# Attention values from a per-image table of column strips in DRAM

## The chip, the cores and the metric

The kernel runs on one core of one Trainium2 chip. A core has TensorE (PE; PEld is its loading of weights), VectorE (DVE), ScalarE (ACT), GpSimd (POOL) and SyncE (SP), which here only issues DMAs; each works through its own instruction queue in order, and they wait for each other by semaphores. The metric is device time in microseconds, as the median of several runs.

## What is computed

Two layers on an image batch x of 2 x 256 x 48 x 48, all in fp32. Layer 0 is a local attention beside a small convolution, on the group-normalised image; layer 1 is a Mamba block and a top-2 mixture of 8 experts on the tokens. The change touches the attention of layer 0 alone:

```python
q = (_c1x1(x, Wq, bq) * HD ** (-0.5)).reshape(b * HEAD, HD, n)
k = _c1x1(x, Wk, bk).reshape(b * HEAD, HD, h, w)
v = _c1x1(x, Wv, bv).reshape(b * HEAD, HD, h, w)
uk = _unfold(jnp.pad(k, rpad, mode='reflect'), KA).reshape(b * HEAD, HD, kk, n)
uv = _unfold(jnp.pad(v, rpad, mode='reflect'), KA).reshape(b * HEAD, HD, kk, n)
att = jnp.einsum('bdn,bdkn->bnk', q, uk + upe[None])
att = jax.nn.softmax(att, axis=-1)
out_att = jnp.einsum('bnk,bdkn->bdn', att, uv).reshape(b, c, h, w)
...
return rate1 * out_att + rate2 * out_conv
```

Every pixel attends to the 7 x 7 window around it (KA = 7), with 4 heads of 64 channels. Since the softmax weights of a pixel add up to 1, the bias bv of the values adds rate1 * bv to each result.

## The kernel before

**Layer 0, one image after the other** (`layer0_image`). `group_norm` writes the normalised image, reflected by 3 pixels on each side, into two tiles `xp` of 128 channels x 54 x 54 (DVE at L221, POOL for the borders at L227 to L232; the reciprocal root `grstd` is POOL's, L162). Matmuls at L272 and L287 make queries and keys, ACT (L277) and DVE (L291) take them out of PSUM.

**Blocks and rounds.** The 48 x 48 queries are cut into 18 blocks of 8 x 16; a block's keys are a window of 14 x 22 = 308 positions of the padded image. `attend` handles a block: POOL copies the block's window of `xp` into a dense tile `win` (L311, once per channel half); PE projects it by Wv in three pieces of 110, 110 and 88 positions (L319), DVE adds the bias on the way out of PSUM into `val` (L323); PE makes the scores of a head pair (L331), DVE adds the mask and takes the maximum (L337); ACT exponentiates (L345), DVE scales by 1/sum and rate1 (L352); for each head pair PE transposes the probabilities (L360), ACT copies them out as `pt` (L364, L367), PE multiplies by `val` (L374), and DVE adds the result into x (L379).

**What sets the order.** Three blocks go through these steps side by side, together with the convolution (`conv_steps`: 36 taps per image of about 2.5 us each on DVE, L248 and L250; half of them write `hid`, half add into x). `interleave` steps all four streams in turn, and six such rounds make an image. The generators give the program order; a scheduler then writes each engine's queue, reordering what does not depend on each other. Taps that add into x and the results at L379 write the same tile, so they keep their program order.

**Buffers.** `bank` is a pool of four PSUM banks (projections, results of L374), `banks` one of two double banks (scores and transposed probabilities in turn). `win`, `val`, `prob` and `pt` have three buffers (NATT). One program matmul in fp32 shows as two records in the trace.

After layer 0 come `mamba` (both images interleaved) and `experts`, which the change does not touch.

Of the kernel before, what the change touches and what calls it, by code (L numbers as in the profile page):

```python
# [40 lines left out]
HP = H + 2 * PAD  # L41
QR, QC = 8, 16
KR, KC = QR + 2 * PAD, QC + 2 * PAD
NKEY = KR * KC
KCH = ((0, 5), (5, 5), (10, 4))
NRB, NCB = H // QR, W // QC
NATT = 3
NEG = -3.0e38

DI, DS, SH = 512, 64, 8  # L50
# [6 lines left out]
E, HID = 8, 1024  # L57
# [12 lines left out]
_VEC = {}  # L70
_n = 0
for _name, _k in (
    ("bq", NH), ("bk", NH), ("bp", 1), ("w1", NH * 9), ("w2", NH * 9), ("norm_w", NH),
    ("gnorm_w", DI // P), ("conv_w", NM * 4), ("conv_b", NM),
):
    _VEC[_name] = (_n, _n + _k)
    _n += _k
# [2 lines left out]
_ROW = {}  # L80
_n = 0
for _name, _k in (
    ("bv", C), ("dt_bias", SH), ("A_log", SH), ("Dp", SH), ("bg", E), ("rate1", 1), ("rate2", 1),
):
    _ROW[_name] = (_n, _n + _k)
    _n += _k
# [32 lines left out]
class Kernel:  # L119
# [45 lines left out]
    def layer0(self, ctx):  # L165
        nc, ins, v, r = self.nc, self.ins, self.v, self.r
        wts = self.pool("l0w", 1, ctx)
        self.xpp = self.pool("xpp", 1, ctx)
        self.att = self.pool("att", NATT, ctx)
        w = {}  # L170
        for k in ("Wq", "Wk", "Wv"):
            w[k] = wts.tile([P, NH, C], F32, name=k)
            nc.scalar.dma_start(w[k], ins[k].rearrange("(h p) o -> p h o", p=P))
        wp = wts.tile([2, P], F32, name="wp")
        nc.scalar.dma_start(wp, ins["Wp"])
        pos = self.xpp.tile([2, HP, HP], F32, tag="kp0", name="pos")
        nc.scalar.dma_start(pos, ins["pos"].rearrange("a (r c) -> a r c", r=HP))

        bq8 = wts.tile([P, NH], F32, name="bq8")
        nc.vector.tensor_scalar(bq8, v["bq"], HD ** -0.5, None, ALU.mult)  # L180
        bkp = wts.tile([P, NH], F32, name="bkp")
        nc.vector.tensor_scalar(bkp, v["bk"], v["bp"], None, ALU.add)
        w2r = wts.tile([P, NH * 9], F32, name="w2r")
        nc.vector.tensor_scalar(w2r, v["w2"], r["rate2"], None, ALU.mult)


        pe = wts.tile([P, HP, HP], F32, name="pe")
        for g in range(6):
            ps = self.bank()
            nc.tensor.matmul(ps[:, : 9 * HP], lhsT=wp, rhs=pos[:, 9 * g : 9 * g + 9, :], start=True, stop=True)  # L190
            nc.scalar.copy(pe[:, 9 * g : 9 * g + 9, :], ps[:, : 9 * HP].rearrange("p (r c) -> p r c", r=9))
        self.l0 = dict(w, bq8=bq8, bkp=bkp, w2r=w2r, pe=pe)
        for b in range(B):
            self.layer0_image(b)
            if b == 0:
                self.scale_weights()
# [65 lines left out]
    def layer0_image(self, b):  # L262
# [3 lines left out]
        for h in range(NH):  # L266
# [28 lines left out]
                )  # L295
            kp.append(kh)

        def blocks(first):
            for i in range(first, NRB * NCB, NATT):
                yield from self.attend(b, i // NCB, i % NCB, xp, q, kp)  # L300

        interleave(*[blocks(i) for i in range(NATT)], self.conv_steps(b, xp))

    def attend(self, b, rb, cb, xp, q, kp):

        nc, l0, att = self.nc, self.l0, self.att
        r0, c0 = rb * QR, cb * QC

        win = att.tile([P, NH, NKEY], F32, tag="win", name="win")
        for k in range(NH):  # L310
            nc.gpsimd.tensor_copy(  # L311
                win[:, k, :].rearrange("p (r c) -> p r c", r=KR), xp[k][:, r0 : r0 + KR, c0 : c0 + KC]
            )
        val = att.tile([P, len(KCH), C], F32, tag="val", name="val")
        for i, (kr, nr) in enumerate(KCH):
            ps = self.bank()
            nk = nr * KC
            for k in range(NH):
                nc.tensor.matmul(  # L319
                    ps[:nk, :C], lhsT=win[:, k, kr * KC : (kr + nr) * KC], rhs=l0["Wv"][:, k, :],  # L320
                    start=k == 0, stop=k == NH - 1,
                )
            nc.vector.tensor_tensor(val[:nk, i, :], ps[:nk, :C], self.r["bv"][:nk, :], ALU.add)  # L323

        prob = att.tile([P, 4, NKEY], F32, tag="prob", name="prob")
        top = self.small.tile([P, 4], F32, tag="top", name="top")
# [27 lines left out]
        for h in range(NH):  # L354
# [24 lines left out]
            nc.vector.tensor_tensor(x, po[:, :P].rearrange("p (r c) -> p r c", r=QR), x, ALU.add)  # L379


    def mamba(self, ctx):
# [468 lines left out]
    def run(self):  # L851
# [8 lines left out]
                nc.sync.dma_start(self.x[b][:, h, :], self.ins["x"][b, h * P : (h + 1) * P, :])  # L860
        self.mamba_weights()
        self.xs = nc.dram_tensor("xs", (NROWS, XW), F32).ap()
        self.acc = nc.dram_tensor("acc", (B * N + P, C), F32).ap()

        self.none = self.const.tile([P, XW], F32, name="none")
# [47 lines left out]
def _arrays(i):  # L913
# [5 lines left out]
    cols = lambda a: a.reshape(-1, P).T  # L919
    taps = lambda a, k: a.reshape(-1, P, k).transpose(1, 0, 2).reshape(P, -1)  # L920
    vec = {
        "bq": cols(l0("bq")), "bk": cols(l0("bk")), "bp": cols(np.tile(l0("bp"), 2)),
        "w1": taps(l0("w1"), 9), "w2": taps(l0("w2"), 9), "norm_w": cols(at("norm_w")),
        "gnorm_w": cols(at("gnorm_w")), "conv_w": taps(at("conv_w"), 4), "conv_b": cols(at("conv_b")),
    }
# [3 lines left out]
         np.broadcast_to(ff("b2")[:, None, :], (E, P, C)),  # L929
         np.broadcast_to(np.eye(E, dtype=np.float32)[:, None, :], (E, P, E))], axis=2)  # L930
    row = {
        "bv": l0("bv"), "dt_bias": at("dt_bias"), "A_log": at("A_log"), "Dp": at("Dp"), "bg": ff("bg"),
        "rate1": l0("rate1").reshape(1), "rate2": l0("rate2").reshape(1),
    }
    out = {
# [27 lines left out]
```

## Time and profile before

| | us |
|---|---|
| median of 3 runs | 2132.05 (2126.8 to 2132.95) |
| the profiled execution's own time | 2135.79 |
| its span in the trace | 2133.7 |
| PE busy in the span | 1745.8 (82%) |
| DVE busy | 1071.7 (50%) |
| POOL busy | 660.3 (31%) |
| ACT busy | 628.7 (29%) |
| granted TensorE clock, mean | 0.859 of full |
| image 0: first Wv matmul to last result | 80.8 to 264.2 |
| image 1: first Wv matmul to last result | 323.8 to 506.6 |
| last tap of layer 0 ends | 517.0 |

How to read the views: a group's row gives the line, engine, operation and tile names, the shapes and the count, then busy time in us and mean ns of one, then how long the engine sat idle just before these instructions and what ended most of that wait. A timeline row gives start and length in us, and in brackets the idle time ahead of it with its releaser. A row of windows gives busy time of each engine in a stretch. DMA rows give the count, the KB of each and the median time from issue to landing.

In layer 0, up to 28 us the inputs are loaded; after that hardly any DMA runs until the Mamba stage.

### The profile page before, as it was taken

To read this page: it belongs to the slowest core of one execution; us is meant where nothing else is said; L and a number is where in the kernel's file an instruction comes from. 1 tells how busy PE (TensorE), PEld (TensorE's weight loads), DVE (VectorE), ACT (ScalarE), POOL (GpSimd) and SP (SyncE) were. 2 spreads that over 40 slices of the span, in tenths; PEclk is the share of its full clock that TensorE was granted. 3 is DMA by queue.
4 is the path that set the end of the run, shared out by engine and by line. 5 is a ranking of instruction groups with operands and counts; after the bars stand their busy time and mean duration, and the time that the engine had idled before them with its cause. 6 is when DMAs were issued, how large, how long until landed. Compare 5 with 4: busy or idle time off the path is not lost. (4 is left out here: it accounts for less than half of the span.)

```text
span 2133.7 us, 22277 instructions
## 1 busy us (share of the span) xinstructions
PE 1745.8 (82%) x7928; PEld 1267.9 (59%) x7928; DVE 1071.7 (50%) x2673; ACT 628.7 (29%) x1449; POOL 660.3 (31%) x579
## 2 busy tenths in 40 slices
PE   5988779785988878887788789339999999999993
PEld 2556536563555554554555545228888888888883
DVE  5678776877666757767567576301111111111111
ACT  1333324332525224243252242002222222222221
POOL 4012040211361743726617446202221212121210
PEclk9999889886977777887777777669999999999995
DMA  5000000000000000000000000036565656565646
GB/s 187 1 1 1 1 0 1 1 1 0 4 11 9 33 8 17 31 10 18 26 9 34 9 18 29 30 148 198 167 193 171 190 175 189 176 184 181 177 136 182
DMA packets 59973, 157.77 MB, mean 74 GB/s; under 512 B 6100, under 2 KB 51158, under 8 KB 53846
## 3 DMA queue, kind: packets, MB, share of 16 engines
q1 hardware_dynamic: 43200, 134.50, 18.2%
q0 software_dynamic: 15840, 21.05, 5.4%
q8 instruction: 63, 1.03, 0.2%
q10 hardware_dynamic: 824, 0.81, 0.1%
q14 instruction: 46, 0.38, 0.1%
HBM read 120.48 MB, written 34.68 MB: 73 GB/s over the span
## 5 line engine op out<-in xcount | busy, mean ns | idle before, releaser
L820 PE MATMUL bank<-ext,wt 128*128 128x256 f32 x1376 | 310.1, 384 | 37.5 <-DVE ext L417 32.9
L820 PEld LDWEIGHTS bank<-ext,wt 128*128 128x128 f32 x1376 | 259.1, 191 | 81.7 <-DVE ext L417 42.8
L835 POOL DMA_INDIRECT acc<-ey,ex x86 | 134.2, 1561 | 560.3 <-DVE ey L833 450.7
L824 ACT ACTIVATE hid<-bank,wt 128x256 f32<-128x256 f32 x344 | 162.7, 473 | 485.8 <-PE bank L820 485.8
L829 PE MATMUL po<-wt,hid 128*128 128x256 f32 x1376 | 304.0, 379 | 0.0
L829 PEld LDWEIGHTS po<-wt,hid 128*128 128x128 f32 x1376 | 261.4, 190 | 35.5
L808 DVE TENSOR_TENSOR own<-ex,wt 128x16 f32<-128x16 f32 x43 | 7.5, 175 | 343.6 <-DMA wt<-in_We 343.6
L832 DVE TENSOR_TENSOR ey<-po,wt 128x256 f32<-128x256 f32 x86 | 36.5, 424 | 209.2 <-PE po L829 209.1
L311 POOL COPY win<-xp 128x308 f32<-128x308 f32 x72 | 56.4, 812 | 259.2 <-PE bank L319 259.2
L637 PE MATMUL banks<-al,cst 128*128 128x512 f32 x144 | 109.4, 881 | 27.4 <-POOL al L609 27.4
L345 ACT ACTIVATE prob<-prob,ntop 128x308 f32<-128x308 f32 x144 | 77.6, 540 | 160.5 <-DVE ntop L342 160.5
L609 POOL TENSOR_TENSOR al<-cst,a 128x1024 f32<-128x1024 f32 x36 | 70.0, 1952 | 134.8 <-DVE a L532 80.2
L360 PE MATMUL banks<-cst,prob 128*110 128x128 f32 (+1 forms) x432 | 76.3, 327 | 41.5 <-DVE prob L352 35.6
L374 PE MATMUL bank<-pt,val 110*64 110x128 f32 (+1 forms) x864 | 93.4, 304 | 14.8 <-ACT pt L364 12.1
L319 PE MATMUL bank<-Wv,win 128*110 128x256 f32 (+1 forms) x432 | 102.7, 386 | 1.6 <-DVE val L323 1.6
L509 DVE SCALAR_TENSOR_TENSOR xc<-raw,vec,xc 128x384 f32<-128x384 f32 x180 | 103.6, 609 | 0.6
L415 PE MATMUL bank<-cst,t 128*128 128x128 f32 x144 | 36.3, 426 | 78.4 <-DVE t L482 49.8
L162 POOL TENSOR_TENSOR lrs<-rs,half 128x1 f32<-128x1 f32 (+1 forms) x48 | 32.9, 685 | 211.2 <-DVE rs L161 126.6
L729 POOL DMA_INDIRECT xs<-u,rows x72 | 79.3, 1102 | 54.2 <-DMA xs<-u,rows 25.4
L374 PEld LDWEIGHTS bank<-pt,val 110*64 110x64 f32 (+1 forms) x864 | 71.9, 149 | 38.2 <-ACT pt L364 18.1
L360 PEld LDWEIGHTS banks<-cst,prob 128*110 128x110 f32 (+1 forms) x432 | 55.6, 152 | 60.9 <-DVE prob L352 41.1
L250 DVE SCALAR_TENSOR_TENSOR x<-hid,w2r,x 128x2209 f32<-128x2209 f32 (+2 forms) x36 | 91.5, 2542 | 0.3
(208 smaller groups left out, 3105.4 us busy)
## 6 DMA issues: line engine op xcount, KB each, us to landing
wt<-in_We SPq DMA_DIRECT2D x43, 2184.0 KB, 8.8
ex<-xs SPq DMA_DIRECT2D x43, 265.0 KB, 2.8
x<-in_x SPq DMA_DIRECT2D x4, 1152.0 KB, 10.7
acc<-x SPq DMA_DIRECT2D x36, 128.0 KB, 2.1
t<-acc SPq DMA_DIRECT2D x12, 384.0 KB, 3.9
out<-o SPq DMA_DIRECT2D x24, 192.0 KB, 3.7
xs<-none SPq DMA_DIRECT2D x15, 265.0 KB, 2.9
acc<-ey,ex POOLq DMA_INDIRECT x86, 3.9
```

What stands on the lines that cost most here:

```text
L250: nc.vector.scalar_tensor_tensor(dst, src, w[:, k : k + 1], dst, ALU.mult, ALU.add)
L319: nc.tensor.matmul(ps[:nk, :C], lhsT=win[:, k, kr * KC : (kr + nr) * KC], rhs=l0["Wv"][:, k, :], start=k == 0, stop=k == NH - 1,)
L345: nc.scalar.activation(prob[:, a, :], prob[:, a, :], AF.Exp, bias=ntop[:, a : a + 1], accum_out=den[:, a : a + 1])
L360: nc.tensor.transpose(ps[: nr * KC, j, i * P : (i + 1) * P], prob[:, 2 * h + j, kr * KC : (kr + nr) * KC], self.ident)
L374: nc.tensor.matmul(po[j * HD : (j + 1) * HD, :P], lhsT=val[:nk, i, a * HD : (a + 1) * HD], rhs=pt[:nk, j, i, :], start=i == 0, stop=i == l ...
L509: nc.vector.scalar_tensor_tensor(xc[:, m, :], raw[:, m, k : k + TB], wc[:, k : k + 1], xc[:, m, :], ALU.mult, ALU.add)
L637: nc.tensor.matmul(pd[:, k, :], lhsT=gt, rhs=al[:, 4 * k : 4 * k + 4, :].rearrange("p s t -> p (s t)"), start=True, stop=True,)
L729: nc.gpsimd.indirect_dma_start(self.xs, bass.IndirectOffsetOnAxis(ap=rows[:, j, k : k + 1], axis=0), u2[:, j, :], None)
L820: nc.tensor.matmul(ps[:, :TR], lhsT=w1[:, k, c * P : (c + 1) * P], rhs=xt[:, k, :], start=k == 0, stop=k == NH - 1,)
L824: nc.scalar.activation(hid[:, c, :], ps[:, :TR], AF.Gelu, bias=b1[:, c : c + 1])
L829: nc.tensor.matmul(po, lhsT=hid[:, c, j * P : (j + 1) * P], rhs=w2[:, c, :], start=c == 0, stop=c == NHC - 1)
L835: nc.gpsimd.indirect_dma_start(self.acc, bass.IndirectOffsetOnAxis(ap=token, axis=0), y[:, j, :], None, compute_op=ALU.add)
```

## The change

Values are no longer projected block by block. A new function `values` runs once per image, after the keys and before the blocks. It takes the 54 x 54 = 2916 padded positions in 23 chunks of 128 (the last of 100), with the positions as the stationary side and Wv moving, two chunks to a PSUM bank. ACT copies a bank into `vout` (two buffers), and SP stores it to a DRAM raster of positions x 256 channels. When 18 image rows of the raster are stored (VR), SP copies them, DRAM to DRAM, into three tables of column strips, one for each of the block columns, 22 positions wide; there a block's 14 x 22 window is one contiguous run. `attend` then loads its three pieces of `val` from the table by three DMAs; `val` gets a fourth buffer. The window copies on POOL, the projection in `attend` and the bias add on DVE go. The bias is added as rate1 * bv when the result is added into x, by one instruction with three operands in place of L379. The broadcast row of constants loses bv's 256 columns, and the column constants gain two.

```diff
+VR = 18
...
+        bv1 = wts.tile([P, NH], F32, name="bv1")
+        nc.vector.tensor_scalar(bv1, v["bv"], r["rate1"], None, ALU.mult)
...
+        self.values(b, xp)
+
...
+    def values(self, b, xp):
+        nc, npos = self.nc, HP * HP
+        flat = [x.rearrange("p r c -> p (r c)") for x in xp]
+        raster = self.vraster[b]
+        windows = [self.vtab[b, cb].rearrange("(r c) d -> r c d", c=KC) for cb in range(NCB)]
+        copied = 0
+        for p0 in range(0, npos, 2 * P):
+            parts = [(p, min(P, npos - p)) for p in range(p0, min(p0 + 2 * P, npos), P)]
+            ps = self.bank()
+            for i, (p, n) in enumerate(parts):
+                for k in range(NH):
+                    nc.tensor.matmul(
+                        ps[:n, i * C : (i + 1) * C], lhsT=flat[k][:, p : p + n],
+                        rhs=self.l0["Wv"][:, k, :], start=k == 0, stop=k == NH - 1,
+                    )
+            out = self.att.tile([P, 2, C], F32, tag="vout", name="vout", bufs=2)
+            if len(parts) == 2 and parts[1][1] == P:
+                nc.scalar.copy(out.rearrange("p i c -> p (i c)"), ps)
+                nc.sync.dma_start(raster[p0 : p0 + 2 * P, :].rearrange("(i p) c -> p i c", p=P), out)
+            else:
+                for i, (p, n) in enumerate(parts):
+                    nc.scalar.copy(out[:n, i, :], ps[:n, i * C : (i + 1) * C])
+                    nc.sync.dma_start(raster[p : p + n, :], out[:n, i, :])
+            while copied < HP and (copied + VR) * HP <= p0 + 2 * P:
+                rows = slice(copied, copied + VR)
+                for cb in range(NCB):
+                    nc.sync.dma_start(
+                        windows[cb][rows],
+                        raster.rearrange("(r c) d -> r c d", c=HP)[rows, cb * QC : cb * QC + KC, :],
+                    )
+                copied += VR
+
     def attend(self, b, rb, cb, xp, q, kp):
...
-        win = att.tile([P, NH, NKEY], F32, tag="win", name="win")
-        for k in range(NH):
-            nc.gpsimd.tensor_copy(
-                win[:, k, :].rearrange("p (r c) -> p r c", r=KR), xp[k][:, r0 : r0 + KR, c0 : c0 + KC]
-            )
-        val = att.tile([P, len(KCH), C], F32, tag="val", name="val")
+        val = att.tile([P, len(KCH), C], F32, tag="val", name="val", bufs=NATT + 1)
         for i, (kr, nr) in enumerate(KCH):
-            ps = self.bank()
-            nk = nr * KC
-            for k in range(NH):
-                nc.tensor.matmul(
-                    ps[:nk, :C], lhsT=win[:, k, kr * KC : (kr + nr) * KC], rhs=l0["Wv"][:, k, :],
-                    start=k == 0, stop=k == NH - 1,
-                )
-            nc.vector.tensor_tensor(val[:nk, i, :], ps[:nk, :C], self.r["bv"][:nk, :], ALU.add)
+            nk, first = nr * KC, (r0 + kr) * KC
+            nc.sync.dma_start(val[:nk, i, :], self.vtab[b, cb, first : first + nk, :])
...
-            nc.vector.tensor_tensor(x, po[:, :P].rearrange("p (r c) -> p r c", r=QR), x, ALU.add)
+            nc.vector.scalar_tensor_tensor(
+                x, po[:, :P].rearrange("p (r c) -> p r c", r=QR), l0["bv1"][:, h : h + 1], x, ALU.add, ALU.add
+            )
...
+        self.vraster = nc.dram_tensor("vraster", (B, HP * HP, C), F32).ap()
+        self.vtab = nc.dram_tensor("vtab", (B, NCB, HP * KC, C), F32).ap()
```

More of the change, by code (lines that the diff above doesn't have):

```diff
@@ L72 @@
 for _name, _k in (
-    ("bq", NH), ("bk", NH), ("bp", 1), ("w1", NH * 9), ("w2", NH * 9), ("norm_w", NH),
+    ("bq", NH), ("bk", NH), ("bv", NH), ("bp", 1), ("w1", NH * 9), ("w2", NH * 9), ("norm_w", NH),
     ("gnorm_w", DI // P), ("conv_w", NM * 4), ("conv_b", NM),
@@ L82 @@
 for _name, _k in (
-    ("bv", C), ("dt_bias", SH), ("A_log", SH), ("Dp", SH), ("bg", E), ("rate1", 1), ("rate2", 1),
+    ("dt_bias", SH), ("A_log", SH), ("Dp", SH), ("bg", E), ("rate1", 1), ("rate2", 1),
 ):
@@ L191, in layer0 @@
             nc.scalar.copy(pe[:, 9 * g : 9 * g + 9, :], ps[:, : 9 * HP].rearrange("p (r c) -> p r c", r=9))
-        self.l0 = dict(w, bq8=bq8, bkp=bkp, w2r=w2r, pe=pe)
+        self.l0 = dict(w, bq8=bq8, bkp=bkp, w2r=w2r, pe=pe, bv1=bv1)
         for b in range(B):
@@ L921, in _arrays @@
     vec = {
-        "bq": cols(l0("bq")), "bk": cols(l0("bk")), "bp": cols(np.tile(l0("bp"), 2)),
+        "bq": cols(l0("bq")), "bk": cols(l0("bk")), "bv": cols(l0("bv")), "bp": cols(np.tile(l0("bp"), 2)),
         "w1": taps(l0("w1"), 9), "w2": taps(l0("w2"), 9), "norm_w": cols(at("norm_w")),
@@ L931, in _arrays @@
     row = {
-        "bv": l0("bv"), "dt_bias": at("dt_bias"), "A_log": at("A_log"), "Dp": at("Dp"), "bg": ff("bg"),
+        "dt_bias": at("dt_bias"), "A_log": at("A_log"), "Dp": at("Dp"), "bg": ff("bg"),
         "rate1": l0("rate1").reshape(1), "rate2": l0("rate2").reshape(1),
```

## The prediction

> **What bounds the kernel now.** The change lies in layer 0, so I first cut the span into stages by the places of the first L287, L319, L331 and L250 in the timelines, and asked for busy time by engine in each stage of image 0. Columns: window and length, then busy us (instructions) of PE, PEld, DVE, ACT, POOL, granted clock, DMA share, GB/s.
>
> ```profile
> 27.00:80.80 53.80, 43.30 (x101) 21.68 (x102) 40.80 (x34) 12.57 (x37) 26.79 (x38) 0.90 0.07 16
> 80.80:128.40 47.60, 43.90 (x299) 30.92 (x298) 29.84 (x119) 22.24 (x70) 5.22 (x12) 1.00 0.00 1
> 128.40:264.20 135.80, 110.44 (x714) 80.40 (x712) 112.12 (x266) 49.81 (x147) 20.53 (x18) 0.85 0.00 1
> ```
>
> Rounds 1 and 2 (three blocks each) are PE's: 43.90 of 47.60 us. Rounds 3 to 6 are DVE's, with the convolution taps: 112.12 of 135.80. The first window is norms and Q/K; there DVE leads at its start, PE later. Image 1 repeats this (47.6 and 135.3 us). DMA is idle. The waits of DVE in rounds 3 to 6 (us, times, longest) say what it does in its 24 idle us:
>
> ```profile
> DVE x L379 <- PE bank L374: 18.7, 12, 3.2
> DVE val L323 <- PE bank L319: 4.5, 10, 0.8
> ```
>
> So 4.5 us go with the value adds, 18.7 wait for attention's last matmul and stay. Then the prices, from the groups of the page and of layer 0's window:
>
> ```profile
> L311 POOL COPY win<-xp 128x308 f32<-128x308 f32 x72 | 56.4, 812 | 259.2 <-PE bank L319 259.2
> L319 PE MATMUL bank<-Wv,win 128*110 128x256 f32 (+1 forms) x432 | 102.7, 386 | 1.6 <-DVE val L323 1.6
> L323 DVE TENSOR_TENSOR val<-bank,row 110x256 f32<-110x256 f32 (+1 forms) x108 | 43.1, 417 | 19.7 <-PE bank L319 19.4
> L364 ACT COPY pt<-banks 110x512 f32<-110x512 f32 x72 | 42.1, 585 | 70.6 <-PE banks L360 70.6
> ```
>
> POOL's 56.4 us wait for PE (259.2 us): hidden. PE rows (start, us) show the pace and what idleness costs; the last is the first row after a PE wait of 7.44 us:
>
> ```profile
> 83.50 1.32 PE L331 MATMUL banks<-kp,q 64*128 64x308 f32 x8
> 84.76 2.84 PE L319 MATMUL bank<-Wv,win 128*110 128x256 f32 x12
> 152.58 4.45 PE L360 MATMUL banks<-cst,prob 128*110 128x128 f32 x18 [7.44 <-DVE prob L352]
> ```
>
> A block's values take 87.53-84.76 = 2.77 us of PE, so 0.231 per matmul record. Last, the nearest transfers (KB each, us to landing):
>
> ```profile
> wt<-in_We SPq DMA_DIRECT2D x43, 2184.0 KB, 8.8
> acc<-x SPq DMA_DIRECT2D x36, 128.0 KB, 2.1
> xs<-none SPq DMA_DIRECT2D x15, 265.0 KB, 2.9
> ```
>
> **The change, per image; t = 0 is its first score matmul.**
>
> (1) *Table pass, +20.3.* 23 chunks of 128 positions by 2 halves are 46 program matmuls, 92 records (L319: 432 records for 216). The new order on PE puts 44 of them (88 records) between the last K matmul and the first score: 88 x 0.231 = 20.3 us, one chunk later. Nothing covers this: the stretch before is already PE's (Q/K matmuls back to back), and DVE's next entries in the new order are the score reductions; the taps that add into x stay where program order puts them. ACT copies a pair of chunks in about 0.59 (L364) and its buffer comes back after an issue (0.5) and landing (2.9, xs row): 4.0 per two pairs, 2.0 a pair against PE's 1.85; with four banks PE keeps its pace. Bounds: 19 to 24.
>
> (2) *Rounds 1 and 2, +2.3.* Removed: 6 blocks x 2.77 = 16.6 us of PE, 18 adds. But PE was also what spaced things; next in line are ACT, SP and the two score banks. By the new orders: scores and their reductions (12 x 0.40 DVE, hand-overs) end at 6.5, exps (0.54 each, 12) at 9.2, three transposed copies (0.95 each) at 12.95. Here ACT has table copies 8, 9, 10. Copy 10 needs the buffer of 8, whose store goes out at 13.6: 13.6+0.5+2.9 = 17.0, done 17.7; two pt copies and table copy 11 end at 20.2. Behind the waiting copy stand those pt copies; PE waits for them. Round 2's scores then start at 20.3, with one of the two score buffers still held by a transposition whose copy stands behind round 2's exps: scores and reductions alternate, 6 x (0.66+0.8+0.4) = 11.2, to 31.5; exps to 33.9; table copy 12 to 34.5. SP now issues block 4's values (the first of round 2), waits for store 12 (37.5), issues the last three strip copies and only then the values of blocks 5 and 6. Behind this wait stand just these loads. The three copies carry 18 x 5632 x 4 B = 405 KB each; 18 rows dealt out two to an engine keep 9 engines busy, at best 16; at wt's rate (2184 KB in 8.8 us on 16, 15.5 KB/us each) three take 4.9 to 8.7 us, and the load 2.1 more: block 5's values come at 44.5 to 48.3, where its product is due at 42.9. I take 46.5, 48.5 for block 6, and round 3's first tap after that block's product, at 49.8. Now the first tap comes 128.37-80.82 = 47.5 after the first round's start: +2.3. Bounds: PE's whole 16.6 gained, or 15 lost if the copies run at half that rate.
>
> (3) *Rounds 3 to 6, -16.6.* 36 adds less at 0.335 (three back to back take 1.07, two 0.74) = 12.1, and the 4.5 of waits. In these rounds PE also loses 33 us, behind DVE, at no gain. What is late next is the 18.7 of L379, untouched. Value loads: four buffers, each released a round ahead, 3 us to load, hidden behind a round of some 30 us; without that cover, 3 us a block. Bounds: 12 (the adds alone) to 20.
>
> (4) *Colder PE, +2.* Where PE idled 7.44 us, the window 150 to 160 shows a granted clock of 0.57 (100 to 110, without gaps: 1.00), and transpositions took 1.53 to 1.60 us (186.11, 251.43) for 0.87 (100.44), products 2.03 (184.15) for 1.15 (101.24). The value matmuls kept PE warm in rounds 1, 2 and 6; scores alone fill 0.66 of every 1.86 us. One cold group of each, (1.55-0.87)+(2.03-1.15) = 1.6, once or twice; I take 2, bounds 0 to 6.
>
> The Trainium skill's page "TensorE: Matmul & The Clock Gate", section "HAM oscillation — how this bites in real kernels", says idle gaps over about 3.4 us put PE back to half clock. By it the score steps of round 2, whose gaps are 1.2 us, would cost nothing and only the first groups after exps would be cold. The trace's 0.57 agrees with the half clock; it shows no gaps as short as those.
>
> (5) *POOL, -1.2.* Before each image's second norm POOL does three window copies (1.22 and 1.21 us at 33.1 and 284.6) that DVE's wait for grstd ends behind. The other 66 copies are hidden.
>
> (6) *Bias and the rest, 0.* L379 becomes a three-operand form: 72 times 0 to 0.06 us (720 ns for 486 elements against 287 for 128: little beyond the length), inside rounds; bv1 and the row load (145 KB less 128) beside the loads of x. 24 stores, 18 strip copies and 108 loads on SP, which has nothing else to issue here.
>
> The Trainium skill's "DMA: Bandwidth & Descriptors", section "Why a DMA increments its semaphore by 16 and not by 1", speaks against the strip copies: the engines used are the largest number up to 16 that divides both slowest dimensions, so 18 rows would use 9. By it the copies stand at the 8.7 us end and the forecast some 3 to 4 us higher. No run before shows a copy from DRAM to DRAM.
>
> **Sum.** 20.3+2.3-16.6+2-1.2 = +6.8 per image, +13.6 for two. The stage end moves the rest one to one: mamba's first transposition waits for the last tap (517.00, L415 after L250). Against the profiled execution: 2135.79 us for a span of 2133.7 (2.1 around it), so 2149.4; that execution is 3.7 above the median 2132.05, so on the median's scale 2145.7, forecast **2146**.
>
> **Rivals.** *All new waits are hidden*: rounds 1 and 2 shrink by PE's 16.6. 20.3-16.6-16.6-1.2 = -14.1, twice: 2132-28 = 2104. For it: PE's 92% there, DMA empty, DVE 63% busy. Against it: ACT's and SP's orders above. It decides where ACT's copy 10 finds its buffer free and three strip copies land within 3.3 us. *An even result*: the table pass and the savings cancel, as when round 2's loads and the clock cost nothing: 20.3-2.2-16.6-1.2, 2133. *Slow strip copies*, slower still: a DRAM-to-DRAM copy at half wt's rate on 9 engines takes 17 us for three; round 1's third block waits 3 more, round 2's second comes at 57 instead of 46.5. +13 per image: 2146+26 = 2172. That 3.3 is 42.9-37.5-2.1; the forecast holds 6.9, and each us more is two in the total. *It doesn't do what it says*: 184 value records instead of 432 are in the new order, so I give this nothing.
>
> **How the numbers follow.** About 0.3% (6.4 us) can be told from no change. Chances: forecast 0.42 (own range 2138 to 2160, from copies at 4.9 to 8.7 and the clock's 0 to 6), slow copies 0.17, even 0.18, hidden 0.23. Hence faster 0.23, same 0.18, slower 0.59. The range 2108 to 2172 takes in half of the hidden case and most of the slow copies; extremes of all terms at once lie outside.
>
> **What will show it.** Step 1: 20 us between K's last matmul and the first score with DVE nearly idle; wrong if taps or reductions fill it. Step 2: ACT waiting for a DMA ahead of a table copy, score records in pairs 1.9 apart in round 2, PE or DVE waiting for a val load there. Step 3: rounds 3 to 6 at about 119 us. Step 4: clock under 1.00 in rounds 1 and 2. Strip copies: landing times of three over 8.7. Rounds 1 and 2 together at 31 us would make the forecast wrong.

## The result and the profile after

The changed kernel took 2138.83 us (median of 4 runs, 2137.61 to 2141.03), the kernel before, run beside it, 2130.86 us (4 runs, 2126.8 to 2132.95): a ratio of 1.0041, 95% interval 1.0022 to 1.0059, slower by 0.4%. Repeated later with ten runs it took 2143.06 us, ratio 1.0037 (1.0024 to 1.0050). The forecast was 2146. The profiled execution took 2137.61 us, 1.8 of them around its span of 2135.8.

First the stages of image 0, cut as before, with one more for the table pass (window and length, then busy us and instructions of PE, PEld, DVE, ACT, POOL, granted clock, DMA share, GB/s):

```profile
23.00:75.66 52.66, 43.90 (x103) 22.39 (x104) 40.88 (x35) 12.71 (x37) 24.47 (x32) 0.90 0.15 38
75.66:94.74 19.08, 19.08 (x89) 16.53 (x87) 0.72 (x1) 4.09 (x7) 0.00 (x0) 1.00 0.47 156
94.74:145.75 51.01, 38.22 (x242) 26.87 (x242) 23.38 (x99) 25.07 (x76) 0.00 (x0) 0.77 0.35 116
145.75:262.90 117.15, 79.17 (x559) 56.18 (x557) 100.64 (x231) 49.24 (x147) 0.00 (x0) 0.75 0.10 31
```

The second line is the price: PE busy for all of its 19.08 us, DVE for 0.72. In the third PE is busy 5.7 us less than in the same rounds before (16.6 us of matmuls are gone, but the others run at a granted clock of 0.77 in place of 1.00), and the stage is 3.4 us longer: PE no longer bounds it. In the fourth DVE does 11.5 us less and the stage is 18.6 us shorter.

DVE's waits in that fourth stage (us, times, longest) and, over the whole run, the groups that answer to L319 and L379:

```profile
DVE x L409 <- PE bank L404: 15.6, 11, 3.3
```

```profile
L324 PE MATMUL bank<-Wv,xp 128*128 128x256 f32 (+1 forms) x184 | 40.4, 379 | 0.0
...
L409 DVE SCALAR_TENSOR_TENSOR x<-bank,bv,x 128x128 f32<-128x128 f32 x72 | 24.5, 348 | 67.9 <-PE bank L404 67.9
```

The waits for value matmuls are gone; the wait for attention's last product (L379 then, L409 now) stays, as forecast. The value matmuls fell from 432 records to 184. The result add went from 287 to 348 ns.

Where rounds 1 and 2 went is read from the timelines of PE, of ACT and of SP's queue (start, us, instruction, what ended a wait before it):

```profile
112.94 0.87 PE L390 MATMUL banks<-cst,prob 128*110 128x128 f32 x6
113.95 0.80 PE L361 MATMUL banks<-kp,q 64*128 64x308 f32 x4
115.74 0.80 PE L361 MATMUL banks<-kp,q 64*128 64x308 f32 x4 [0.99 <-DVE top L367]
117.53 0.80 PE L361 MATMUL banks<-kp,q 64*128 64x308 f32 x4 [0.99 <-DVE top L367]
119.31 1.40 PE L361 MATMUL banks<-kp,q 64*128 64x308 f32 x4 [0.99 <-DVE top L367]
121.98 1.40 PE L361 MATMUL banks<-kp,q 64*128 64x308 f32 x4 [1.28 <-DVE top L367]
124.37 1.40 PE L361 MATMUL banks<-kp,q 64*128 64x308 f32 x4 [0.99 <-DVE top L367]
...
140.76 0.40 PE L404 MATMUL bank<-pt,val 110*64 110x128 f32 x2 [2.09 <-DMA val<-vtab]
```

```profile
110.22 0.59 ACT L330 COPY vout<-bank 128x512 f32<-128x512 f32 x1 [1.78 <-DMA vraster<-vout]
...
129.90 0.35 ACT L334 COPY vout<-bank 100x256 f32<-100x256 f32 x1
130.28 0.58 ACT L394 COPY pt<-banks 110x512 f32<-110x512 f32 x1
```

```profile
130.28 0.27 SPq L335 DMA_DIRECT2D vraster<-vout  x1
130.59 1.15 SPq L353 DMA_DIRECT2D val<-vtab  x3
132.13 2.16 SPq L339 DMA_DIRECT2D vtab<-vraster  x3
134.39 15.60 SPq L353 DMA_DIRECT2D val<-vtab  x15
```

The six score pairs of round 2 alternate with DVE's reductions, one pair at a time: 11.8 us (113.95 to 125.77) for 6.6 us of matmuls. They have one of the two score buffers: the other holds the transposition of 112.94, round 1's last, which ACT copies out only at 130.28, behind round 2's exps. The value loads of blocks 5 and 6 stand on SP behind the last three strip copies, and PE waits for block 5's until 140.76.

The two profiled executions differ by only 1.8 us, because that of before had begun late: its position rows landed at 14.55 us. In the thirteen other profiles of this study they land between 10.94 and 11.91, with the small row constants and with the large ones (11.55, the kernel before with early taps), so the late start does not come from the large constants and looks like chance. So stages are compared from that landing on. To Mamba's first norm it is 503.0 us in the kernel before, 508.8 in the changed one and 515.5 in its repeat: 5.8 and 12.5 us more. What follows varies without a change of its code: from that norm to the first expert matmul the kernels of this study took 902 to 914 us.

### The profile page after: what moved, and what is told of

The parts are those of the page before. It is cut to its first block, busy times and chain, and to the rows that moved or that the text cites. A ratio compares the mean times of both kernels' runs of the same rounds, so it can differ in the third digit from the quotient of the medians.

```text
span 2135.8 us, 21835 instructions
## 1 busy us (share of the span) xinstructions
PE 1715.5 (80%) x7680; PEld 1247.8 (58%) x7680; DVE 1036.5 (49%) x2566; ACT 641.7 (30%) x1473; POOL 603.9 (28%) x507
## 5 line engine op out<-in xcount | busy, mean ns | idle before, releaser
L861 PEld LDWEIGHTS po<-wt,hid 128*128 128x128 f32 x1376 | 261.4, 190 | 35.5
L390 PE MATMUL banks<-cst,prob 128*110 128x128 f32 (+1 forms) x432 | 84.3, 354 | 48.0 <-DVE prob L382 44.8
L404 PE MATMUL bank<-pt,val 110*64 110x128 f32 (+1 forms) x864 | 94.9, 322 | 18.9 <-ACT pt L394 12.8
L390 PEld LDWEIGHTS banks<-cst,prob 128*110 128x110 f32 (+1 forms) x432 | 61.5, 164 | 71.5 <-DVE prob L382 50.8
L404 PEld LDWEIGHTS bank<-pt,val 110*64 110x64 f32 (+1 forms) x864 | 76.4, 161 | 39.9 <-ACT pt L394 17.7
L447 PE MATMUL bank<-cst,t 128*128 128x128 f32 x144 | 36.3, 426 | 76.2 <-DVE t L514 49.9
L361 PE MATMUL banks<-kp,q 64*128 64x308 f32 x288 | 61.2, 531 | 33.1 <-DVE top L367 32.9
L473 PE MATMUL bank<-xn,win 128*128 128x384 f32 x240 | 86.8, 521 | 0.0
```

The lines of the kernel that those rows point to most:

```text
L390: nc.tensor.transpose(ps[: nr * KC, j, i * P : (i + 1) * P], prob[:, 2 * h + j, kr * KC : (kr + nr) * KC], self.ident)
L404: nc.tensor.matmul(po[j * HD : (j + 1) * HD, :P], lhsT=val[:nk, i, a * HD : (a + 1) * HD], rhs=pt[:nk, j, i, :], start=i == 0, stop=i == l ...
L473: self.nc.tensor.matmul(ps, lhsT=lhs(k), rhs=rhs(k), start=k == 0, stop=k == NH - 1)
L861: nc.tensor.matmul(po, lhsT=hid[:, c, j * P : (j + 1) * P], rhs=w2[:, c, :], start=c == 0, stop=c == NHC - 1)
```

## The experiments

The stages in all profiles (us; two numbers are images 0 and 1). "K to tap" runs from the start of VectorE's last K add to the first tap that adds into x, so table pass and rounds 1 and 2 together; "tap to add" from there to the last result add, rounds 3 to 6; "layer 0" from the landing of the position rows to Mamba's first norm.

| kernel | K to tap | tap to add | layer 0 | median us | ratio to before |
|---|---|---|---|---|---|
| before | 47.4, 47.4 | 135.5, 134.9 | 503.0 | 2129 to 2133 | 1 |
| changed | 69.9, 69.0 | 116.8, 117.6 | 508.8 | 2138.8 | 1.0041 (1.0022 to 1.0059) |
| changed, repeated | 70.3, 69.4 | 119.9, 120.6 | 515.5 | 2143.1 | 1.0037 (1.0024 to 1.0050) |
| no table for image 1 | 70.1, 39.3 | 119.8, 120.0 | 484.6 | 2110.1 | 0.9901 (0.9888 to 0.9914) |
| raster loads | 64.5, 63.4 | 119.8, 119.9 | 504.0 | 2124.6 | 0.9977 (0.9965 to 0.9989) |
| three table buffers | 76.2, 74.8 | 118.7, 118.7 | 525.0 | 2146.5 | 1.0077 (1.0064 to 1.0090) |
| bias alone | 47.4, 50.0 | 135.6, 135.6 | 506.2 | 2132.3 | 1.0015 (1.0004 to 1.0027) |
| strips of 16 rows | 62.6, 61.9 | 118.5, 117.7 | 497.2 | 2129.8 | 0.9979 (0.9970 to 0.9989) |
| strips of 16 and 2 | 72.5, 73.0 | 117.8, 117.1 | 516.1 | 2147.1 | 1.0080 (1.0064 to 1.0095) |
| pass spread | 44.9, 44.9 | 122.9, 124.3 | 473.8 | 2108.2 | 0.9878 (0.9858 to 0.9898) |
| early taps, changed | - | - | 458.7 | 2087.6 | 0.9781 (0.9763 to 0.9799) |
| early taps, before | - | - | 532.6 | 2161.0 | 1.0129 (1.0110 to 1.0148) |
| early taps, raster loads | - | - | 451.3 | 2081.0 | 0.9755 (0.9728 to 0.9783) |
| early taps, pass spread | - | - | 465.2 | 2099.3 | 0.9838 (0.9821 to 0.9855) |

The theory at the start of the experiments: the table pass stands alone on the path (19 us an image); rounds 3 to 6 pay back about as much; rounds 1 and 2 gain nothing from the 16.6 us of PE work they lost, because the engines' order there holds them. Rivals: the transfers are the loss; the pass only displaces idle time; the moved bias or its row constants are.

### No table for image 1

```diff
-        self.values(b, xp)
+        if b == 0:
+            self.values(b, xp)
...
-            nc.sync.dma_start(val[:nk, i, :], self.vtab[b, cb, first : first + nk, :])
+            nc.sync.dma_start(val[:nk, i, :], self.vtab[0, cb, first : first + nk, :])
```

> The changed kernel, but image 1 makes no table: its blocks load image 0's (image 1's values are left out of the computation). Theory: the table pass stands alone on the path, 19.1 us between image 1's last K matmul and its first score, and the rest of the loss is in rounds 1 and 2 (store waits, strip copies ahead of loads, cold PE). Then the first score of image 1 follows K at once, and rounds 1 and 2 shrink from 50.1 us to 38 to 44: in all 25 to 31 us less than the changed kernel's 2138.8, 2108 to 2114. Rival, that the pass only displaces idle time (without it rounds 1 and 2 wait elsewhere): at most 10 us less, 2129 or above. Rival, that the pass costs what it shows and nothing else: rounds 1 and 2 stay at 50, 2119.7.

Measured: 2110.07 us, inside the theory's 2108 to 2114. PE's timeline of image 1:

```profile
317.82 7.50 PE L292 MATMUL bank<-xp,Wk 128*128 128x486 f32 x18
325.25 1.32 PE L362 MATMUL banks<-kp,q 64*128 64x308 f32 x8
...
345.61 1.32 PE L362 MATMUL banks<-kp,q 64*128 64x308 f32 x8
346.86 1.15 PE L405 MATMUL bank<-pt,val 110*64 110x128 f32 x12
347.94 1.32 PE L362 MATMUL banks<-kp,q 64*128 64x308 f32 x8
```

The first scores follow K at once, so the pass costs its 19 us in full, and rounds 1 and 2 take 39.45 us in place of 50.15. Round 2's scores start 20.4 us after the first, no earlier than in the changed kernel (19.3), but come two pairs at a time between round 1's products, without a wait, and end at 351.6: 6.0 us in place of 11.8. So of the other 11 us that the pass costs only 1 is its own matmuls (the last chunk): the rest is what its last copies and stores do to the order and the waits of rounds 1 and 2. Even without them these rounds gain only 8 us against the kernel before (39.3 for 47.4 from K to the first tap), half of the 16.6 us of matmuls that they lost.

### Loads from the raster, without strip tables

```diff
-            nk, first = nr * KC, (r0 + kr) * KC
-            nc.sync.dma_start(val[:nk, i, :], self.vtab[b, cb, first : first + nk, :])
+            nk, first = nr * KC, r0 + kr
+            nc.sync.dma_start(
+                val[:nk, i, :],
+                self.vraster[b].rearrange("(r c) d -> r c d", c=HP)[first : first + nr, c0 : c0 + KC, :],
+            )
```

with the 18 strip copies and their table left out.

> The changed kernel without the strip tables and their 18 copies from DRAM to DRAM: each block loads its pieces from the raster itself, 5 or 4 rows of 22 positions. Theory: the strip copies cost only round 2's late loads (waits of 2.1 and 0.8 us on PE, 6.9 on DVE), so 2 to 5 us an image go, 2129 to 2135 (changed kernel 2138.8), and the 19.1 us between K and the first score stay. Rival, that the transfers are the whole loss: 8 us or more go, at or below the 2130.9 of before. Rival, that the loads were hidden all along: 2137 to 2140.

Measured: 2124.56 us, faster than both kernels: by its number the rival, and not the theory. By stages the gain is 5.4 and 5.6 us between K and the first tap, against 2 to 5 expected, and rounds 1 and 2 take 43.2 us. But the order differs too: ScalarE makes all of its table copies ahead of round 1's exps, half of them after a wait for a store (K to the first score is 21.2 us, 20.1 in image 1), and round 2's scores come two pairs at a time. The run alone does not tell the missing copies from the changed order.

### Three table buffers

```diff
-            out = self.att.tile([P, 2, C], F32, tag="vout", name="vout", bufs=2)
+            out = self.att.tile([P, 2, C], F32, tag="vout", name="vout", bufs=3)
```

> The changed kernel with three table buffers in place of two (no more fit). Theory: ScalarE's wait of 1.78 us for a store in round 1, with transposed copies behind it, goes, and round 2 starts 1 to 3 us earlier; 2 to 4 us in all, if round 2's strip copies do not take it back: 2135 to 2139. Rival, that this wait is the centre of round 1's stall (round 2's scores started 19.2 us after the first): 10 us or more, below 2130.

Measured: 2146.49 us, slower than the changed kernel; both expectations fail. PE in round 1, and SP's queue:

```profile
111.34 0.65 PE L404 MATMUL bank<-pt,val 110*64 110x128 f32 x4
121.94 2.83 PE L404 MATMUL bank<-pt,val 88*64 88x128 f32 x20 [9.95 <-DMA val<-vtab]
```

```profile
110.27 0.39 SPq L331 DMA_DIRECT2D vraster<-vout  x1
110.83 2.16 SPq L339 DMA_DIRECT2D vtab<-vraster  x3
113.03 0.98 SPq L331 DMA_DIRECT2D vraster<-vout  x2
114.12 0.37 SPq L335 DMA_DIRECT2D vraster<-vout  x1
114.54 2.83 SPq L353 DMA_DIRECT2D val<-vtab  x4
```

ScalarE's wait for a store (1.27 us, at the last table copy) no longer delays a transposed copy, but round 1's last value loads now stand behind the second set of strip copies and three stores, and PE waits 9.95 us for them in round 1 where it waited 0.51 in the changed kernel. A buffer more moved the stall, and made it longer.

### The bias alone, in the kernel before

```diff
-            nc.vector.tensor_tensor(val[:nk, i, :], ps[:nk, :C], self.r["bv"][:nk, :], ALU.add)
+            nc.vector.tensor_copy(val[:nk, i, :], ps[:nk, :C])
...
-            nc.vector.tensor_tensor(x, po[:, :P].rearrange("p (r c) -> p r c", r=QR), x, ALU.add)
+            nc.vector.scalar_tensor_tensor(
+                x, po[:, :P].rearrange("p (r c) -> p r c", r=QR), l0["bv1"][:, h : h + 1], x, ALU.add, ALU.add
+            )
```

> The kernel before with only the bias moved: values copied without it, the small row constants, the result add in three-operand form. Theory: 72 result adds cost 0.06 us more each, 48 of them in rounds 3 to 6 where VectorE leads, so 0 to 4 us more than before: 2131 to 2135; and the earlier start in the changed kernel's profile (position rows landing by 10.9 us in place of 14.6) is chance of the first loads, which the other runs of this call show by spreading between the two. Rival, that the smaller row constants bring the start forward by 3.6 us: 2127 to 2130, and an early landing in every kernel with the small row.

Measured: 2132.26 us beside 2129.03, within the theory's 0 to 4 us; layer 0 is 3.2 us longer. The profile does not put this on the result add. In rounds 3 to 6, 0.1 and 0.7 us longer, VectorE's 1.5 us more of work are made up by less waiting (for L374 17.0 us in place of 18.7 in image 0). The rest, 2.6 us from K to tap in image 1, is a stretch in which PE has half its clock, while the same instructions ran at full clock in the kernel before (windows as above, first before, then the bias alone):

```profile
339.00:346.00 7.00, 6.34 (x62) 5.17 (x61) 2.44 (x9) 4.54 (x13) 0.00 (x0) 1.00 0.01 2
335.50:342.50 7.00, 6.75 (x38) 5.32 (x37) 2.01 (x7) 3.78 (x12) 0.00 (x0) 0.51 0.01 2
```

The start is as early as in the other kernels (position rows at 11.26 us) and brings no time.

### The changed kernel repeated

> The changed kernel once more, unchanged. Theory: layer 0 is nearly fixed and the rest varies: the four profiled kernels of the runs so far needed 902.8 to 910.6 us from the end of layer 0 to the first expert matmul though their code there is the same. So layer 0 ends again at 518 to 521 us with the position rows landing at about 11, and the median lies 5 to 10 us above before. Rival, that layer 0 itself varies: its end moves by more than 3 us.

Measured: 2143.06 us, 10.0 above the kernel before by the medians and 7.9 by the ratio, the upper end of the range; but layer 0 ended at 526 us and not at 518 to 521, 6.7 us longer with the same code, most of it in rounds 3 to 6 (116.8 and 117.6 us, then 119.9 and 120.6): the rival is right in this. Differences below some 4 us an image between single profiles prove nothing here by themselves.

### Early taps, in the changed kernel and in the one before

In both kernels, ahead of the table pass (before: ahead of the blocks):

```diff
+        conv = self.conv_steps(b, xp)
+        for _ in range(14):
+            next(conv)
...
-        interleave(*[blocks(i) for i in range(NATT)], self.conv_steps(b, xp))
+        interleave(*[blocks(i) for i in range(NATT)], conv)
```

> The changed kernel with the first half of the convolution (its 9 taps on half 0 and the 9 that add into x) put ahead of the table pass in program order. Theory: VectorE stands idle for 19 us beside the table pass and leads in rounds 3 to 6; 9 taps of 2.54 us move out of rounds 3 to 6 into the pass, some 19 us an image, of which a little is lost where the second half's first taps now stand between the reductions of round 1: 12 to 20 us an image, 24 to 40 in all, 2099 to 2115. Rival, that rounds 3 to 6 are held by the latency from reductions to products and not by VectorE's work: under 8 us an image, above 2123.

> The kernel before with the same early taps. Its rounds 1 and 2 have 17.8 us an image in which VectorE idles, but scattered between value adds and reductions on TensorE's path. Theory: it gains 8 to 16 us an image there, 2097 to 2113 (before: 2129 to 2131), less than the changed kernel gains. Rival, that taps of 2.5 us between the value adds and reductions hold TensorE up by about as much: 0 to 6 us in all, 2123 to 2131. It also keeps the large row constants: if these set the start, its position rows land at about 14.5 as in before's profile; if that was chance, nearer to 11.

Measured: 2087.57 us in the changed kernel, 51 to 56 less than its two medians without, more than the 24 to 40 expected; 2161.04 us in the kernel before, 28 more, a loss that neither expectation had. The expectation overlooked where the taps went from: of the 50 us that layer 0 is shorter, 13.5 and 17.8 lie between K and the last result of each image, and 10 more per image behind that result, where the changed kernel's last four taps (10.28 us from 508.71 on) ran with no block left beside them. VectorE of the changed kernel beside the table pass:

```profile
77.86 18.03 DVE L255 SCALAR_TENSOR_TENSOR x<-hid,w2r,x 128x2256 f32<-128x2256 f32 x7
95.81 0.47 DVE L370 CUSTOM_DVE_ANT_0 prob<-banks,cst 128x308 f32<-128x308 f32 x1
```

Seven taps fill the 18 us and the reductions start without a wait. PE and DVE of the kernel before, with the same edit:

```profile
83.54 1.11 PE L322 MATMUL bank<-Wv,win 128*110 128x256 f32 x4 [0.17 <-DVE val L326]
86.30 1.10 PE L322 MATMUL bank<-Wv,win 128*88 128x256 f32 x4 [1.65 <-DVE val L326]
...
119.97 1.60 PE L363 MATMUL banks<-cst,prob 128*110 128x128 f32 x6 [13.17 <-DVE prob L355]
```

```profile
83.07 0.42 DVE L326 TENSOR_TENSOR val<-bank,row 110x256 f32<-110x256 f32 x1
83.41 2.51 DVE L250 SCALAR_TENSOR_TENSOR x<-hid,w2r,x 128x2209 f32<-128x2209 f32 x1
85.83 0.42 DVE L326 TENSOR_TENSOR val<-bank,row 110x256 f32<-110x256 f32 x1
86.17 2.56 DVE L250 SCALAR_TENSOR_TENSOR x<-hid,w2r,x 128x2256 f32<-128x2256 f32 x1
```

Here a tap of 2.5 us stands between every two value adds, whose banks PE waits for (3.5 us in all); the longer waits follow, 8.0 us for reductions with taps between them, and 13.17 for the scaled probabilities, ahead of which VectorE makes five taps of the second half. The same taps, nine of each image, are worth 51 us where TensorE works without VectorE, and cost 28 where it needs VectorE after every 1 to 2 us of matmuls.

### The pass spread over the rounds

On the raster loads; the values become a stream that yields twice after each pair of chunks.

```diff
-        self.values(b, xp)
+        table = self.values(b, xp)
+        for _ in range(6):
+            next(table)
...
-        interleave(*[blocks(i) for i in range(NATT)], self.conv_steps(b, xp))
+        interleave(table, *[blocks(i) for i in range(NATT)], self.conv_steps(b, xp))
```

> The raster loads (no strip tables), and the table pass cut up: three pairs of chunks, the rows that round 1 needs, ahead of the blocks, the other nine one pair in every second step of the blocks. Theory: of the 19 to 21 us between K and the first score about 14 go into idle TensorE time of the rounds; rounds 1 and 2 keep about 43 to 46 us, rounds 3 to 6 about 118: 10 to 16 us an image against the raster kernel (2124.6), so 2093 to 2105, below both the kernel before and the changed one. Rival, that the pieces hold up the blocks' own matmuls and ScalarE copies as much as they save: 2118 to 2130.

Measured: 2108.22 us, just above the theory's range and below the rival's. Layer 0 is 30 us shorter than with the raster loads alone in the two profiles; the whole kernel is 16 us shorter by the medians and 21 by the ratios. Image 0:

```profile
77.80:84.50 6.70, 6.70 (x34) 5.62 (x32) 0.59 (x1) 1.76 (x3) 0.00 (x0) 1.00 0.26 81
84.50:122.50 38.00, 34.10 (x251) 23.82 (x251) 22.96 (x99) 24.57 (x74) 0.00 (x0) 1.00 0.29 93
122.50:245.50 123.00, 87.17 (x606) 62.94 (x604) 101.00 (x231) 52.02 (x152) 0.00 (x0) 0.79 0.12 39
```

Rounds 1 and 2 with part of the pass in them take 38.0 us, PE busy for 34.1 of them at full clock: the time that the changed kernel's rounds 1 and 2 idle away was there to be filled. Rounds 3 to 6 pay 3 to 4 us for the rest of the pass.

### Strips of 16 rows, and of 16 and 2

```diff
-VR = 18
+VR = 16
...
-            while copied < HP and (copied + VR) * HP <= p0 + 2 * P:
-                rows = slice(copied, copied + VR)
+            while copied < HP and min(copied + VR, HP) * HP <= p0 + 2 * P:
+                rows = slice(copied, min(copied + VR, HP))
```

> The changed kernel with strip copies of 16 rows in place of 18 (16, 16, 16 and 6 rows, twelve copies an image in place of nine). Theory: in the trace of the kernel with three table buffers, three strip copies alone keep the DMA share at 0.57 and move 215 GB/s of reads and writes as the profile counts them, as if 9 of 16 engines worked; with 16 rows a set runs at a share near 1, takes 3.5 us in place of 5.7, and round 2's wait for values (2.1 and 0.8 us on TensorE) shrinks: 1 to 4 us an image, 2132 to 2140 (changed kernel 2138.8 and 2143.1). Rival, that the copies are bound by the memory and not by their engines: the share stays near 0.57 and the time within 3 us. Rival, that only the order of ScalarE's table copies matters, which this edit shifts as well: rounds 1 and 2 differ by more than 5 us with the share unchanged.

```diff
-                rows = slice(copied, copied + VR)
                 for cb in range(NCB):
-                    nc.sync.dma_start(
-                        windows[cb][rows],
...
+                    for rows in (slice(copied, copied + 16), slice(copied + 16, copied + VR)):
+                        nc.sync.dma_start(
+                            windows[cb][rows],
```

> The changed kernel with each strip copy of 18 rows given as two, 16 rows and 2 rows. In layer 0 TensorE, VectorE and ScalarE keep the changed kernel's order, instruction for instruction (the kernel with strips of 16 rows did not: there ScalarE's table copies and TensorE's scores and products had another order as well); on SyncE only the doubled copies, and block 4's three value loads now behind the last set. Theory, that the order of the engines held rounds 1 and 2: the sets run on all 16 engines and finish sooner, but rounds 1 and 2 stay within 3 us of 51.0 and 50.2, and the time at 2135 to 2142. Rival, that the speed of the copies held them: rounds 1 and 2 go to 43 to 46 as with strips of 16 rows (43.7 and 43.0), 2126 to 2132.

Measured: strips of 16 rows 2129.75 us, faster than the theory's range and just faster than before; strips of 16 and 2 rows 2147.12 us, slower than the changed kernel and above both ranges. The first shortens rounds 1 and 2 to 43.7 and 43.0 us, the second lengthens them to 53.6 and 54.1 us. PE's round 2 in the second, image 0:

```profile
115.28 0.80 PE L361 MATMUL banks<-kp,q 64*128 64x308 f32 x4
117.06 0.80 PE L361 MATMUL banks<-kp,q 64*128 64x308 f32 x4 [0.99 <-DVE top L367]
...
125.70 1.40 PE L361 MATMUL banks<-kp,q 64*128 64x308 f32 x4 [0.99 <-DVE top L367]
...
141.03 2.39 PE L404 MATMUL bank<-pt,val 110*64 110x128 f32 x16 [2.73 <-DMA val<-vtab]
```

With the changed kernel's order the six single pairs take the same 11.8 us (115.28 to 127.10), whatever the copies do. With strips of 16 rows the same scores take 8.2 us (116.67 to 124.88), most of them two pairs at a time with products between, as in image 1 without a table: the edit happened to bring that order, and the copies' speed cannot be credited with it. In every profile that has the pass in one piece and the taps in their old place, the place of round 1's last transposed copy goes with it. Where ScalarE makes it behind round 2's exps (16 to 18 us after these scores start), they take 11.8 to 13.3 us: the changed kernel and its repeat, three buffers, strips of 16 and 2, image 0 of the kernel with one table. Where it is made before or just as they start (raster loads, strips of 16 rows, image 1 without a table), they take 6.0 to 8.2 us.

The first expectation rests on a mistaken reading of the trace: the steady stretch at 215 GB/s is value loads and stores, whose packets are of 1 KB; a strip copy's packets are whole rows of 22.5 KB. Read by those, from the first one's start to the last one's end, the six sets of three 18-row copies in the changed kernel (54 rows, 1.22 MB) take 6.0 to 7.2 us, and the six sets of 16-row copies (1.08 MB) 4.1 to 5.1. But the six sets of copies split into 16 and 2 rows take 6.7 to 7.4 us, no less than whole: in image 0 six copies take 3.4 to 4.8 us to issue where three took 2.2 to 2.4. So the split kernel did not get the faster sets that were expected, and it does not test the rival; what faster copies alone are worth stays open.

### Early taps with raster loads, pass whole and spread

Both edits above together, on the raster loads.

> Early taps and raster loads together, the table pass in one piece. Theory: the two gains lie in different places (taps beside the pass; strip copies and late table copies in rounds 1 and 2), so they add: the early taps gave 51 to 55 us, the raster loads 14, of which rounds 1 and 2 with taps in them keep about half: 2073 to 2083. Rival, that with early taps VectorE leads from the first round and the transfers are hidden: 2085 to 2092, as with early taps alone (2087.6).

> Early taps, raster loads, and the table pass cut into the rounds. Theory: TensorE then holds 6.8 us between K and the first score, and the early taps (23 us) lose most of their cover and stand between the reductions of round 1; but VectorE's whole work of the stretch, some 135 us an image, now bounds it, against 169 us from K to the end with early taps alone: 10 to 15 us an image less is possible, and half of it is likely: 2062 to 2082. Rival, that reductions held up by taps of 2.5 us idle TensorE as in the kernel before with early taps (28 us lost there): 2095 to 2125, worse than the one-piece pass.

Measured: 2081.02 us with the pass whole, the lowest median here, 2.45% below the one before (2.2 to 2.7), inside the theory's range; the runs spread from 2069.95 to 2087.88, and the interval overlaps that of early taps alone. With the pass spread 2099.34 us, as the rival had it: the taps lost their cover (K to the first score is 5.4 us) and layer 0 is 14 us longer than with the pass whole. The two cures do not add: the exposed pass is worth having as soon as VectorE has taps to do beside it.

## Why the prediction was right, and where its sizes were off

The forecast's case held: slower, by an exposed pass that rounds 3 to 6 pay back and rounds 1 and 2 do not. Its +13.6 us came out as +8.0 by the medians and +8.7 by the ratio (4.7 to 12.6), in the repeat as +10.0 and +7.9 (5.1 to 10.7), and as +5.8 and +12.5 in layer 0 of the two profiles. So the mechanism was right and the size too large. In the first profile the terms below add up to 19.1+3.5-18.7 = 3.9 us for image 0 and 19.1+2.6-17.3-1.0 = 3.4 for image 1; with 1.5 us less from the position rows to image 0's last K add that is the 5.8.

- *Table pass, +20.3.* Measured 19.1 in both images, and 19 lost with it when image 1 made no table. The mis-sized term is the 0.231 us a record: it came from a group of 12 records in the kernel before, while 88 records in one piece take 19.08/88 = 0.217. That is 1.2 us an image too much.
- *Rounds 1 and 2, +2.3, with up to +2 of colder PE.* Measured 51.01-47.5 = +3.5 and +2.6 (repeat +3.9 and +3.0). The chain held within 1.6 us at every step: exps' end at t=9.2 (103.94 less 94.74, forecast 9.2), table copy 10 started after its wait at 15.5 (buffer free at 17.0), round 2's scores at 19.2 (20.3), table copy 12 done at 35.5 (34.5), block 5's product at 46.0 (values 46.5), first tap at 51.0 (49.8). The alternation of scores and reductions on one free score buffer, forecast from the new order, is the six single pairs; to the last reduction they took 12.8 us (11.2), the last three at half clock.
- *Rounds 3 to 6, -16.6.* Measured -18.7 and -17.3 in the first profile, -15.6 and -14.4 in the repeat: the forecast lies between the two. DVE's work fell by the adds, its waits for value matmuls went, L409's 15.6 us (18.5 in the repeat) stayed.
- *Colder PE, +2.* It is in the two terms above and no run measures it by itself. The forecast put it on transpositions and products after long waits; it also struck the scores. The granted clock of image 0's round 2, windows of the changed kernel:

```profile
118.00:119.30 1.30, 0.32 (x4) 0.00 (x0) 0.88 (x4) 1.30 (x6) 0.00 (x0) 0.90 0.43 149
119.30:121.00 1.70, 1.40 (x4) 0.51 (x4) 0.94 (x4) 0.66 (x4) 0.00 (x0) 0.50 0.59 205
121.00:124.00 3.00, 1.40 (x4) 0.51 (x4) 2.16 (x11) 1.38 (x5) 0.00 (x0) 0.50 0.01 3
```

The clock fell to 0.50 amid the score pairs, after gaps of 0.99 us with PE busy for 0.80 of every 1.79 us, and a pair went from 0.80 to 1.40 us. By the starts of the pairs, 1.79 us apart at full clock and then 2.67, 2.39 and 2.39, that is about 2 us of round 2 (an estimate; DVE's scaling between the pairs has some 0.3 of it). The rule of "TensorE: Matmul & The Clock Gate", section "HAM oscillation — how this bites in real kernels", that gaps over some 3.4 us bring half clock, would by itself have kept it at full; the measurement decides, and the prediction was right not to lean on the rule. Its remark that the trace of before has no gaps this short was wrong: rounds 1 and 2 there have gaps of 0.46 to 0.73 us at a clock of 1.00, but with PE busy for 92% of the time. Nor do such gaps decide it by themselves: the stretch of image 1 that ran at 1.00 in the kernel before ran at 0.51 for 7 us with the bias alone, after gaps of 0.50 and 0.73 us in both.

- *POOL, -1.2.* The stretch from image 0's last result add to image 1's last K add is 60.1 us in the two kernels that have window copies there (before, and the bias alone) and 59.1 in all eight without them that have the taps in the same place: -1.0. At the start of image 0 nothing of the kind can be told from the spread.
- *Bias, 0.* The result add cost 0.061 us more, the top of the bound, and in the kernel before the bias alone cost 3 us (ratio 1.0015, 1.0004 to 1.0027). The profile of that kernel gives the add less than 1 us an image and the rest to a stretch of half clock, so what the term should have been stays open between 0 and +3.
- *Strip copies.* From the first issue of the last set (132.13) to the end of its last packet (139.63) it took 7.5 us, where 6.9 stood in the chain, and PE had the load behind it 1.1 us later (2.1): 8.6 us in place of 9.0 by two errors that nearly cancel, so that block 5's time was partly luck. The rival of slow copies did not come true. The rivals that all new waits are hidden, or that it comes out even, fall with PE's 2.09 and ScalarE's 1.78 us and with the intervals.

What remains open: what the clock costs in all in rounds 1 and 2; what faster strip copies alone would be worth; and why rounds 3 to 6 and the Mamba stage vary by several us between runs of the same code (in image 0's rounds 3 to 6 the granted clock was 0.75 in the first profile and 0.71 in the repeat, which fits, but shows no cause).

## What to carry to other kernels

A matmul pass that is moved ahead of a loop is exposed unless another engine has work to do beside it: look for work of the next bottleneck that depends on nothing in the loop (here taps, 51 us), or cut the pass and feed it to the loop as it needs it (16 to 21 us). Work taken from the busiest engine of a stage gains nothing until the next wait in line is read from the new order: here a score buffer whose copy is queued behind exps took the place of PE. And an order that is good beside one kernel can be bad beside another: the same early taps gave 51 us after the change and cost 28 before it.

## What the runs showed of the hardware

Copies from DRAM to DRAM depend on their number of rows. The rows of a strip copy, packets of 22.5 KB, start in groups: nine at a time in the copies of 18 rows, sixteen in those of 16 rows, six in those of 6. One group each, from the last set of the changed kernel (135.7 to 136.4 us) and the second of the kernel with 16-row strips (97.5 to 98.3 us):

```profile
DMA packets 18, 0.20 MB, mean 290 GB/s; under 512 B 9, under 2 KB 9, under 8 KB 9
```

```profile
DMA packets 32, 0.36 MB, mean 451 GB/s; under 512 B 16, under 2 KB 16, under 8 KB 16
```

Nine rows with nine packets of 4 bytes in the first, sixteen with sixteen in the second. The rule of "DMA: Bandwidth & Descriptors", section "Why a DMA increments its semaphore by 16 and not by 1", by which 18 rows use 9 engines and 16 rows 16, agrees with these groups. But the rate does not grow in step: these two sets move 1.22 MB in 6.0 us and 1.08 MB in 4.1 us, 202 and 264 GB/s, 1.3 times as much where 16/9 would be 1.78, since a packet takes 1.13 us in the second and 0.93 in the first. A strip copy of 18 rows takes 0.67 to 0.90 us to issue on SP and its parts of 16 and 2 rows mostly 0.5 to 0.7 each, so splitting a copy to use more engines costs there what it may gain.
